# A two-layer graph network on one core: layer 1 in pairs of blocks, another form of the complex products, and the sums of h taken one group earlier

## The chip, the cores and the metric

One core of one Trainium2 chip. The metric is device time in microseconds (us): the median of nine executions, and for the question where the time goes, one profiled execution with a record of every instruction. TensorE (PE in profiles, PEld for its weight loads) multiplies matrices into PSUM, VectorE (DVE) and ScalarE (ACT) read PSUM and do element-wise work, GpSimd (POOL) does element-wise work on SBUF and issues DMAs, SyncE (SP) issues DMAs. Every engine works through its own instructions in the order in which they were recorded, and waits on semaphores for the others.

## The reference, cut to what matters

x is 128 samples x 128 nodes x 256 features, adj a 0/1 adjacency for each sample; all is float32.

```python
# layer 0
h = max(layernorm(x), 0)
y = bn2(conv1d(relu(bn1(conv1_w @ h)), conv2_w, 17 taps, pad 8))   # along the nodes
x_conv = relu(y + h)
s = h @ w_se.T + b_se
x_nmp = (exp(-dist(s, s)) * mask) @ relu(h @ w_msg.T + b_msg)      # mask is adj
gi, gh = [x_conv, x_nmp] @ w_ih.T + b_ih, h @ w_hh.T + b_hh
r, z = sigmoid(gi_r + gh_r), sigmoid(gi_z + gh_z)
n = tanh(gi_n + r * gh_n)
x = x + (1 - z) * n + z * h
# layer 1: five groups of nodes with 25, 9, 7, 6, 6 members, all among nodes 0 to 24
h = max(layernorm(x), 0)
for g, idx in enumerate(GROUPS):
    A = normalised(adj[:, idx][:, :, idx] + I)
    out_g = relu(A @ (relu(A @ (h[:, idx] @ W1[g]) + b1[g]) @ W2[g]) + b2[g])
    x[:, idx] += softmax(fusion_w)[g] * out_g
```

Layer 1 touches only the 25 nodes that are in a group; W1[g] is 256 x 512, W2[g] 512 x 256.

## The kernel before, in words

The 128 samples are worked on in groups of four (q = 0 to 31, `GB` = 4), eight groups make a batch (`bat`, 0 to 3) of layer 0's convolution, and four groups make a block of 16 samples (`blk`, 0 to 7, `SB` = 16) of layer 1.

Layer 0's convolution with 17 taps is done through a Fourier transform over 48 points. `stage_a(q)` normalises four samples, turns them (hT, also written to DRAM as hTd), multiplies with conv1_w (pc, L396) and transforms (pf, L409) into X. `stage_b(bat)` multiplies, for each of 24 frequencies f, the real and imaginary parts of a batch's X with those of the taps. A complex product is made of three real ones: per frequency twelve matmul instructions of 256 columns, two products into the bank pa and one into pb (L500). A float32 matmul is two instructions on TensorE. The taps' transforms come from DRAM (wfd, L486), GpSimd adds the third factors (xs, wf; L494, L495), and after the products ACT copies pa out (pac, L519) and DVE makes real and imaginary part with three operations (L523 to L525). GpSimd writes y to DRAM (yd, L528). The cosines and sines that the taps are multiplied with are the constants of `_fourier` (L89).

`stage_n(q)` loads hT and the adjacency and makes the neighbour sums xm (pse, pm, pd, px: L571 to L616); for the first eight groups this was done early and is only loaded. `stage_c(q)` is the gates: it transforms y back (pi, L673) into xc, and multiplies hT, xm and xc with the gate weights (p, L694) with a fast scheme of seven products for two by two blocks. That scheme needs sums of the quarters of each input: `sums` (L546 to L554) makes four of 256 columns on DVE, th from hT, tm from xm, tc from xc. `stage_c` uses th ready made if `TH` holds it, and makes it at its head otherwise (L665). TH of the next group is made behind the last update with the bank pg (L757 to L760), provided that the next group is in `IN`, that is, that its stage_n is complete. At the end tanh (ACT, L788) and six GpSimd operations (d and z, L791 to L794) give the new state, po (L807) turns it back, and DVE adds it to x. Nodes 0 to 31 of the result go to DRAM for layer 1 (x1d, L819), the others to the output; the last block's stay in SBUF (`direct`, L801).

Layer 1 works on blocks. `prepare(blk)` loads the small adjacency (aj), makes the normalised matrices: b1 with five adds on GpSimd (L917; eight instructions), dg on DVE (L922), pa, pdg, pg and pr4 on TensorE (L928 to L960), giving ac and r4. `rows_of_x` loads x1 (L900), takes moments and normalises (L275 to L283, a power on GpSimd at L278, the maximum with 0 on GpSimd at L894) into x1h. `block(blk)` aggregates (py, L979; yz, L981 and L982), multiplies with W1 of each group (`first`: ph, L996, 16 x members columns) and with W2 (`second`: pz, L1005), turns (pzt, L1026), aggregates again (pg2, L1038), and adds the fused result to x1 (pfu, L1047, L1049); GpSimd stores it (L1058). W1[g] is loaded anew for each block and group with two buffers (L878); W2 is loaded once as a whole (`setup_1`).

The order in which instructions are recorded is planned. Stages are generators: each yields the TensorE time it has just recorded and a delay before it should go on. A `Lane` holds stages with a weight, up to `ahead` of them at a time; `Order.run` always goes on with the lane whose recorded TensorE time, divided by its weight, is smallest, among those that are due. First a lane of stage_a, with tap weights beside it; then stage_b(0); then the lane of gates (stage_n and stage_c, weight 1) beside the remaining stages a and b (0.5); and from there to the end the gates beside layer 1 (L1083). When gates are used up, the rest of layer 1 is recorded alone. Conditions such as `blk - 1 in B1_DONE` concern the recording only. PSUM has three banks for gates (`pgat`) and five for all else (`ptmp`), taken in turn.

```python
    groups = Lane([stage(q) for q in range(NQ) for stage in (stage_n, stage_c)], ahead=2)
    side = Lane(first, weight=0.5)
    order.run(groups, side, until=side)
    order.run(groups, Lane(second, ahead=2, weight=0.4))
```

Of the kernel before, what the change touches and what calls it, by code (L numbers as in the profile page):

```python
# [59 lines left out]
def _fourier():  # L60
# [26 lines left out]
    for f in range(1, NF + 1):  # L87
        th = 2 * np.pi * ((f * t) % F) / F
        tap[:, f], tap[:, NF + 1 + f] = np.cos(th), np.sin(th)  # L89
# [118 lines left out]
def kernel(ctx: ExitStack, tc: tile.TileContext, x, adj, consts, vecs, w_se, conv1_w,  # L208
# [265 lines left out]
    def stage_b(bat):  # L474
# [31 lines left out]
        for f in range(NF + 1):  # L506
            if f + 2 <= NF:
                load_w(f + 2)
            if f < NF:
                add(f + 1)  # L510
            y = xf.tile([P, 2, D], FP, tag="y", name=f"y{bat}_{f}")
            pa = ptmp.tile([P, 2, D], FP, tag="tmp", name=f"pa{bat}_{f}")
            for s in range(2):
                product(pa[:, s], lambda k: X[:, k, 2 * f + s], f, s)
            if f == 0:
                nc.vector.tensor_copy(y, pa)
            else:
                pac = xf.tile([P, 2, D], FP, tag="pac", name=f"pac{bat}_{f}", bufs=2)
                nc.scalar.activation(pac, pa, AF.Copy)  # L519
                pb = ptmp.tile([P, D], FP, tag="tmp", name=f"pb{bat}_{f}")  # L520
                xs = XS.pop(f)
                product(pb, lambda k: xs[:, k], f, 2)
                nc.vector.tensor_sub(y[:, 0], pac[:, 0], pac[:, 1])  # L523
                nc.vector.tensor_add(pac[:, 0], pac[:, 0], pac[:, 1])
                nc.vector.tensor_sub(y[:, 1], pb, pac[:, 0])  # L525
            WF.pop(f)
            if late is not None:
                nc.gpsimd.dma_start(out=yd[bat][:, 2 * f - 2:2 * f], in_=late)  # L528
            late = y
            yield 1.7 if f == 0 else 2.6, 1.0  # L530
# [13 lines left out]
    TH = {}  # L544
# [91 lines left out]
    def stage_n(q):  # L636
        if q < BQ:
# [4 lines left out]
            yield 0.0, 4.0  # L642
        else:
# [3 lines left out]
            yield 0.0, 4.0  # L647
            xm = LATE["fr"].tile([P, 2, 512], FP, tag="xnmp", name=f"xnmp{q}", bufs=2)
# [3 lines left out]
    def stage_c(q):  # L652
# [99 lines left out]
        for dc in range(2):  # L752
# [6 lines left out]
            if dc and q + 1 in IN:  # L759
                TH[q + 1] = sums("th", q + 1, IN[q + 1][0])  # L760
# [64 lines left out]
    S, B1_DONE, P_DONE, Y_DONE = {}, set(), set(), set()  # L825

    def setup_1():
# [13 lines left out]
        S["w2"] = weight(pool, W2, [P, 5, 4, D], "g (k p) o -> p g k o", "w2", nc.sync)  # L841
        S["ac"] = [pool.tile([P, SB // 2, RP], FP, name=f"ac{i}") for i in range(2)]
        r4 = S["r4"] = [pool.tile([P, QS, GB, NR], FP, name=f"r4{i}") for i in range(2)]
        S["yz"] = pool.tile([P, 2, SB, RP], FP, name="yz")
# [29 lines left out]
    def load_w1(n):  # L874

        if n < NBLK * NG:
            S["w1", n] = S["pool"].tile([P, 2, HID], FP, tag="w1", name=f"w1_{n}", bufs=2)
            nc.sync.dma_start(out=S["w1", n], in_=W1[n % NG].rearrange("(k p) o -> p k o", p=P))  # L878

    def rows_of_x(blk, wait=True):  # L880

        ready = all(q in C_DONE for q in range(blk * QS, (blk + 1) * QS))
        if blk in S or not (wait or ready and blk - 1 in Y_DONE):
            return
        while not (all(q in C_DONE for q in range(blk * QS, (blk + 1) * QS))
                   and blk - 1 in Y_DONE):
# [9 lines left out]

    def load_x1(blk):
# [5 lines left out]
    def prepare(blk):  # L903

        while not (blk - 1 in P_DONE and blk - 2 in {-2, *B1_DONE}):
            yield 0.0, 1.0
        pool, pool2, b1 = S["pool"], S["pool2"], S["b1"]
        ac, r4 = S["ac"][blk % 2], S["r4"][blk % 2]
# [3 lines left out]
        if blk not in X1 and all(q in C_DONE for q in range(blk * QS, (blk + 1) * QS)):  # L912
            load_x1(blk)
# [55 lines left out]
    def block(blk):  # L969
        while not (blk in P_DONE and blk - 1 in B1_DONE):  # L970
            yield 0.0, 0.5
        pool, yz, b2row, s2w = S["pool"], S["yz"], S["b2row"], S["s2w"]
        w2, ac, r4 = S["w2"], S["ac"][blk % 2], S["r4"][blk % 2]
        x1, x1h = X1.pop(blk), S.pop(blk)

        for q in range(QS):
            py = ptmp.tile([P, 2, GB, NR], FP, tag="tmp", name=f"py{blk}_{q}")
            for cc in range(2):
                nc.tensor.matmul(py[:, cc], x1h[:, q, cc * P:(cc + 1) * P],  # L979
                                 r4[:, q].rearrange("p j r -> p (j r)"), start=True, stop=True)  # L980
            nc.vector.tensor_copy(yz[:, 0, q * GB:(q + 1) * GB, :NR], py[:, 0])  # L981
            nc.scalar.activation(yz[:, 1, q * GB:(q + 1) * GB, :NR], py[:, 1], AF.Copy)  # L982
            yield 0.75, 0.0 if q < QS - 1 else 1.5
        Y_DONE.add(blk)

        hs = {}

        def first(g):
            n, o = SIZES[g], OFFS[g]
            w1 = S.pop(("w1", blk * NG + g))  # L990
            hh = hs[g] = pool.tile([P, 4, SB, n], FP, tag="hh0" if g == 0 else "hh",
                                   name=f"hh{blk}_{g}", bufs=1 if g == 0 else 2)
            for m in range(4):
                ph = ptmp.tile([P, SB, n], FP, tag="tmp", name=f"ph1{blk}_{g}_{m}")
                for k in range(2):
                    nc.tensor.matmul(ph, w1[:, k, m * P:(m + 1) * P],  # L996
                                     yz[:, k, :, o:o + n], start=(k == 0), stop=(k == 1))
                nc.scalar.activation(hh[:, m], ph, AF.Relu, bias=v("b1", g * 4 + m))

        def second(g):  # L1000
            n, o = SIZES[g], OFFS[g]
            for cc in range(2):
                pz = ptmp.tile([P, SB, n], FP, tag="tmp", name=f"pz1{blk}_{g}_{cc}")
                for m in range(4):
                    nc.tensor.matmul(pz, w2[:, g, m, cc * P:(cc + 1) * P], hs[g][:, m],  # L1005
                                     start=(m == 0), stop=(m == 3))
                nc.vector.tensor_copy(yz[:, cc, :, o:o + n], pz)

        for g in range(NG + 1):
            if g < NG:  # L1010
                first(g)
                yield 5.5 if g == 0 else 1.95, 0.0
            if g:
                second(g - 1)
                yield 5.5 if g == 1 else 1.95, 0.0 if g < NG else 1.0
            if g < NG:
                load_w1(blk * NG + g + 2)
# [3 lines left out]
        def turn(q):  # L1021
            pz = ptmp.tile([P, 2, D], FP, tag="tmp", name=f"pzt{blk}_{q}")
# [6 lines left out]
            zt = zts[q] = pool.tile([P, 2, D], FP, tag="zt", name=f"zt{blk}_{q}", bufs=3)  # L1029
            nc.scalar.activation(zt, pz, AF.Copy)  # L1030

        def gather(q):
            zt = zts[q]
            pg2 = ptmp.tile([P, 2, D], FP, tag="tmp", name=f"pg2{blk}_{q}")
            for a in range(2):
                for s in range(2):
                    rows = slice(s * RP, (s + 1) * RP)
                    nc.tensor.matmul(pg2[rows, a], ac[rows, 2 * q + a], zt[rows, a],  # L1038
                                     start=True, stop=True)
            nc.vector.tensor_tensor(zt, pg2, b2row[:, None, :].to_broadcast([P, 2, D]), ALU.add)  # L1040
            nc.scalar.activation(zt, zt, AF.Relu)

        def fuse(q):
            zt = zts.pop(q)
            pf = ptmp.tile([P, D], FP, tag="tmp", name=f"pfu{blk}_{q}")
# [3 lines left out]
            nc.vector.tensor_add(x1[:, q], x1[:, q], pf)  # L1049

        for what, q in ((turn, 0), (turn, 1), (turn, 2), (gather, 0), (gather, 1), (fuse, 0),
                        (turn, 3), (gather, 2), (fuse, 1), (gather, 3), (fuse, 2), (fuse, 3)):
            what(q)
            if (what, q) == (gather, QS - 1):
                B1_DONE.add(blk)
            yield {turn: 0.45, gather: 0.9, fuse: 0.5}[what], 0.5
        for j in range(GB):
            nc.gpsimd.dma_start(  # L1058
                out=out[blk * SB:(blk + 1) * SB, :WIDE].rearrange("(q j) n c -> j n q c", j=GB)[j],
                in_=x1[j * WIDE:(j + 1) * WIDE])  # L1060
# [17 lines left out]
    for blk in range(NBLK):  # L1078
        second += [prepare(blk), block(blk)]
# [3 lines left out]
    order.run(groups, Lane(second, ahead=2, weight=0.4))  # L1083
# [41 lines left out]
```

## Time and profile before

| | us |
|---|---|
| median of nine executions | 2243.55 (2239.39 to 2257.99) |
| the profiled execution, its own time | 2243.55 |
| its span, first to last instruction | 2241.8 |
| L500, L694 (all inputs): complex and gate products, TensorE busy | the largest groups; 186.0 for pa, 95.4 for pb |
| L996 + L1005, layer 1's products, TensorE busy | 113.1 + 110.1 |
| stretch 2185 to 2242, TensorE busy | 43.12 of 57 |
| W2's load issued | at 1366.4, 2560 KB |

The profile gives for each engine the time in which it was busy. A matmul's record reaches from its start to the modelled end of its results, so neighbouring records overlap; the distance between starts is the pace. In groups of instructions, "out<-in" are the tiles by name, then come partitions x elements, the count, the busy time, the mean of one in ns, and the idle time in front of them with what ended it. The chain of waits goes back from the last instruction to what released each step. Times in the timeline count from the start of the span.

### The profile page before, as it was taken

Reading aid. Unit: us, or ns where it says so; the run is one execution under the profiler, and the core shown is the slowest. Engines: PE = TensorE matmul, PEld = TensorE weight load, DVE = VectorE, ACT = ScalarE, POOL = GpSimd, SP = SyncE. Lnnn points to the kernel's source line nnn. Section 1 sums busy time; section 2 is a strip of 40 time slices with the busy share of each in tenths; the row PEclk is TensorE's granted clock in tenths of the full one; section 3 lists DMA queues with packets and bytes.
Section 4 is the critical chain, followed back from the end, with each engine's and each line's share of the span. In section 5 each row is a group of like instructions: output and inputs, shape, how many; then the busy total and the mean of one; then the engine's idle time right before and its main releaser. Section 6 shows DMA issues by size and latency. Waiting matters only on the chain.

```text
span 2241.8 us, 31926 instructions
## 1 busy us (share of the span) xinstructions
PE 2154.1 (96%) x11820; PEld 1761.6 (79%) x11820; DVE 1337.0 (60%) x2843; ACT 717.9 (32%) x1455; POOL 810.9 (36%) x978
## 2 busy tenths in 40 slices
PE   6998999999999999999999998999999999999997
PEld 3577778888888888888888887787877878878775
DVE  4556656576557676666666665665655665655442
ACT  2432223322234433333333332233333333333232
POOL 2226503365632245542225454423223323222320
PEclk9998989999999999999999999999999999999999
DMA  9786543454533344432315444323212222221221
GB/s 174 234 275 212 187 117 92 133 182 154 158 111 85 104 136 141 147 119 89 103 47 175 137 146 137 77 76 76 76 57 86 65 59 79 80 74 45 69 73 48
DMA packets 193982, 259.72 MB, mean 116 GB/s; under 512 B 21981, under 2 KB 157154, under 8 KB 192290
## 3 DMA queue, kind: packets, MB, share of 16 engines
q1 hardware_dynamic: 165682, 175.89, 27.2%
q0 software_dynamic: 27312, 81.03, 11.7%
q8 instruction: 94, 1.54, 0.3%
q10 hardware_dynamic: 832, 0.75, 0.2%
q14 instruction: 62, 0.51, 0.1%
HBM read 178.44 MB, written 79.17 MB: 115 GB/s over the span
## 4 chain that ended last, share of the span: by engine, by line
PE 83%; DVE 7%; DMA 4%; issue 2%; ACT 2%; POOL 2%; SPq 1%; DVEq 0%; ACTq 0%; POOLq 0%
PE p L694 32%; PE pa L500 7%; PE pg L755 5%; PE pc L396 5%; PE pz L1005 4%; PE ph L996 4%; PE pm L591 4%; PE pi L673 4%; PE pf L409 3%; PE pb L500 3%; PE px L616 2%; DMA hTd<-hTa 1%; PE pg L1038 1%; PE py L979 1%; PE ph L383 1%
## 5 line engine op out<-in xcount | busy, mean ns | idle before, releaser
L500 PE MATMUL pa<-wf,X 128*128 128x256 f32 x768 | 186.0, 386 | 4.8 <-DVE y L525 4.8
L791 POOL TENSOR_TENSOR d<-hT,r 128x512 f32<-128x512 f32 x64 | 86.5, 1351 | 239.2 <-ACT r L788 206.5
L278 POOL TENSOR_TENSOR rs<-rs,cst 128x4 f32<-128x4 f32 x40 | 41.3, 1032 | 358.8 <-DVE rs L277 343.7
L500 PEld LDWEIGHTS pa<-wf,X 128*128 128x128 f32 x768 | 147.3, 193 | 29.8 <-DVE y L525 6.5
L694 PE MATMUL p<-tc,wrz 128*128 128x256 f32 x512 | 152.9, 380 | 4.0 <-DVE tc L551 4.0
L694 PE MATMUL p<-tm,wrz 128*128 128x256 f32 x512 | 152.4, 379 | 1.6 <-DVE tm L551 1.6
L694 PE MATMUL p<-th,wrz 128*128 128x256 f32 x512 | 153.7, 382 | 0.0
L396 PE MATMUL pc<-c1w,hTa 128*128 128x256 f32 x512 | 130.5, 401 | 8.8 <-ACT hTa L385 8.8
L396 PEld LDWEIGHTS pc<-c1w,hTa 128*128 128x128 f32 x512 | 100.1, 200 | 39.2 <-ACT hTa L385 15.9
L495 POOL TENSOR_TENSOR wf<-wf 128x512 f32<-128x512 f32 x92 | 125.3, 1362 | 11.8 <-DMA wf<-wfd 11.8
L494 POOL TENSOR_TENSOR xs<-X 128x256 f32<-128x256 f32 x92 | 69.0, 750 | 165.3 <-PE pb L500 160.6
L673 PEld LDWEIGHTS pi<-cst,yt 96*128 96x128 f32 x1024 | 123.2, 196 | 4.7 <-issue 3.1
L673 PE MATMUL pi<-cst,yt 96*128 96x64 f32 x1024 | 121.9, 278 | 2.7 <-DMA yt<-yd 2.7
L755 PE MATMUL pg<-hT,whn 128*128 128x512 f32 x256 | 122.6, 605 | 0.0
L591 PE MATMUL pm<-wmsg,hT 128*128 128x256 f32 x512 | 121.3, 381 | 0.0
L694 PE MATMUL p<-hT,wrz 128*128 128x256 f32 x384 | 120.4, 396 | 0.0
L519 ACT ACTIVATE pac<-pa 128x512 f32<-128x512 f32 x92 | 54.7, 595 | 197.9 <-PE pa L500 189.3
L523 DVE TENSOR_TENSOR y<-pac 128x256 f32<-128x256 f32 x92 | 55.4, 603 | 102.2 <-ACT pac L519 98.8
L996 PE MATMUL ph<-yz,w 128*128 128x96 f32 (+3 forms) x640 | 113.1, 332 | 3.4 <-DVE yz L981 2.8
L591 PEld LDWEIGHTS pm<-wmsg,hT 128*128 128x128 f32 x512 | 96.4, 190 | 23.8 <-issue 11.0
L694 PEld LDWEIGHTS p<-tc,wrz 128*128 128x128 f32 x512 | 96.8, 190 | 19.3 <-DVE tc L551 6.4
L1005 PE MATMUL pz<-hh,w 128*128 128x96 f32 (+3 forms) x640 | 110.1, 327 | 1.7 <-DVE aT L608 1.7
(205 smaller groups left out, 4818.6 us busy)
## 6 DMA issues: line engine op xcount, KB each, us to landing
wf<-wfd SPq DMA_DIRECT2D x192, 256.0 KB, 3.2
yd<-y POOLq DMA_DIRECT2D x96, 256.0 KB, 2.6
yt<-yd SPq DMA_DIRECT2D x64, 384.0 KB, 3.7
hT<-hTd SPq DMA_DIRECT2D x40, 512.0 KB, 5.3
w<-in_W SPq DMA_DIRECT2D x40, 512.0 KB, 3.8
xa<-in_x SPq DMA_DIRECT2D x128, 128.0 KB, 4.0
hTd<-hTa POOLq DMA_DIRECT2D x32, 512.0 KB, 4.2
xt<-in_x SPq DMA_DIRECT2D x128, 128.0 KB, 3.2
```

The lines of the kernel that those rows point to most:

```text
L396: nc.tensor.matmul(pc[:, i], hT[:, k, (2 * h + i) * N:(2 * h + i + 1) * N], c1w[:, k], start=(k == 0), stop=(k == 1))
L409: nc.tensor.matmul(pf[:, i, :F * NB], h1[:, 2 * h + i, k * P:(k + 1) * P], fwd, start=True, stop=True)
L494: nc.gpsimd.tensor_tensor(XS[f], X[:, :, 2 * f], X[:, :, 2 * f + 1], ALU.add)
L495: nc.gpsimd.tensor_tensor(WF[f][:, :, 2], WF[f][:, :, 0], WF[f][:, :, 1], ALU.add)
L500: nc.tensor.matmul(ps, xk(k), WF[f][:, k, s], start=(k == 0), stop=(k == 1))
L591: nc.tensor.matmul(pm[:, i], hT[:, k, j * N:(j + 1) * N], wmsg[:, k], start=(k == 0), stop=(k == 1))
L673: nc.tensor.matmul(pc[:, co, a * 64:(a + 1) * 64], yt[:, a, co * P:(co + 1) * P], inv[:HB], start=True, stop=True)
L694: nc.tensor.matmul(ps[:, m], w[:, i, k, m * P:(m + 1) * P], factor(i, x, t), start=first and j == 0, stop=last and j == len(n) - 1)
L755: nc.tensor.matmul(pg, whn[:, k, dc * P:(dc + 1) * P], hT[:, k], start=(k == 0), stop=(k == 1))
L791: nc.gpsimd.tensor_sub(d, hT[:, dc], r[:, dc])
L996: nc.tensor.matmul(ph, w1[:, k, m * P:(m + 1) * P], yz[:, k, :, o:o + n], start=(k == 0), stop=(k == 1))
L1005: nc.tensor.matmul(pz, w2[:, g, m, cc * P:(cc + 1) * P], hs[g][:, m], start=(m == 0), stop=(m == 3))
```

## The change

Four things are changed.

1. Layer 1 works on pairs of blocks (`blocks(sb)`, 32 samples). Groups 1 to 4 are multiplied for both blocks at once; group 0, with 25 members, still half by half[...]. W2 is loaded group by group with two buffers, like W1, and both once for each pair. `ac` has three buffers, `yz` is twice as large. An x1 tile is loaded only when the block two before has been fused (`x1_there`), and block k's prepare needs blocks k - 2 aggregated and k - 3 gathered. The store of a block's result stands at its last fuse.
2. The complex products: pa now holds imaginary part times one factor and real part times the other, the constants of `_fourier` are sums and differences of cosine and sine, ACT copies pb (`kk`) and not pa, and one DVE operation makes y = 2 pa - kk.
3. The condition for making th of the next group is that its hT has been requested (`HT`), not that its stage_n is complete.
4. The share of layer 1 beside the gates is 0.48 instead of 0.4 of theirs.

```diff
-        tap[:, f], tap[:, NF + 1 + f] = np.cos(th), np.sin(th)
+        tap[:, f] = -(np.cos(th) + np.sin(th)) / 2
+        tap[:, NF + 1 + f] = (np.sin(th) - np.cos(th)) / 2
...
-                product(pa[:, s], lambda k: X[:, k, 2 * f + s], f, s)
+                product(pa[:, s], lambda k: X[:, k, 2 * f + (s if f == 0 else 1 - s)], f, s)
...
-                pac = xf.tile([P, 2, D], FP, tag="pac", name=f"pac{bat}_{f}", bufs=2)
-                nc.scalar.activation(pac, pa, AF.Copy)
                 pb = ptmp.tile([P, D], FP, tag="tmp", name=f"pb{bat}_{f}")
                 xs = XS.pop(f)
                 product(pb, lambda k: xs[:, k], f, 2)
-                nc.vector.tensor_sub(y[:, 0], pac[:, 0], pac[:, 1])
-                nc.vector.tensor_add(pac[:, 0], pac[:, 0], pac[:, 1])
-                nc.vector.tensor_sub(y[:, 1], pb, pac[:, 0])
+                kk = xf.tile([P, D], FP, tag="kk", name=f"kk{bat}_{f}", bufs=2)
+                nc.scalar.activation(kk, pb, AF.Copy)
+                nc.vector.scalar_tensor_tensor(y, pa, 2.0, kk[:, None].to_broadcast([P, 2, D]),
+                                               op0=ALU.mult, op1=ALU.subtract)
...
+            HT[q] = hT
...
-            if dc and q + 1 in IN:
-                TH[q + 1] = sums("th", q + 1, IN[q + 1][0])
+            if dc and q + 1 in HT:
+                TH[q + 1] = sums("th", q + 1, HT.pop(q + 1))
...
         for n in range(2):
             load_w1(n)
-        S["w2"] = weight(pool, W2, [P, 5, 4, D], "g (k p) o -> p g k o", "w2", nc.sync)
-        S["ac"] = [pool.tile([P, SB // 2, RP], FP, name=f"ac{i}") for i in range(2)]
+            load_w2(n)
+        S["ac"] = [pool.tile([P, SB // 2, RP], FP, name=f"ac{i}") for i in range(3)]
...
+    def x1_there(blk):
+
+        return (all(q in C_DONE for q in range(blk * QS, (blk + 1) * QS))
+                and blk - 2 in {-2, -1, *F_DONE})
...
+        def first(g, half=None):
+
             n, o = SIZES[g], OFFS[g]
-            w1 = S.pop(("w1", blk * NG + g))
+            bs = slice(0, 2 * SB) if half is None else slice(half * SB, (half + 1) * SB)
+            nb = bs.stop - bs.start
+            w1 = S["w1", sb * NG + g]
...
-                                     yz[:, k, :, o:o + n], start=(k == 0), stop=(k == 1))
+                                     yz[:, k, bs, o:o + n], start=(k == 0), stop=(k == 1))
...
+        yield from aggregate(pair[0])
+        yield first(0, 0)
+        yield from aggregate(pair[1])
+        yield second(0, 0)
+        yield first(0, 1)
+        yield first(1)
+        yield second(0, 1)
+        for g in range(2, NG):
+            yield first(g)
+            yield second(g - 1)
+        yield second(NG - 1)[0], 1.0
...
-    for blk in range(NBLK):
-        second += [prepare(blk), block(blk)]
+    for sb in range(NBLK // 2):
+        second += [prepare(2 * sb), prepare(2 * sb + 1), blocks(sb)]
...
-    order.run(groups, Lane(second, ahead=2, weight=0.4))
+    order.run(groups, Lane(second, ahead=2, weight=0.48))
```

## The prediction, made before the result was known

> **What bounds the kernel now.** I read the page's first lines, then the chain of waits, the table by stage, the groups with shapes kept apart, and the timeline of the end.
>
> ```profile
> span 2241.8 us, 31926 instructions
> PE 2154.1 (96%) x11820; PEld 1761.6 (79%) x11820; DVE 1337.0 (60%) x2843; ACT 717.9 (32%) x1455; POOL 810.9 (36%) x978
> PEclk9998989999999999999999999999999999999999
> PE 83%; DVE 7%; DMA 4%; issue 2%; ACT 2%; POOL 2%; SPq 1%; DVEq 0%; ACTq 0%; POOLq 0%
> ```
>
> TensorE is busy nearly everywhere and carries 83% of the chain that ended last. But busy is not pace, so I take the pace from the chain in order of time (start, length, what):
>
> ```profile
> 606.13 10.36 PE p L694 x48
> 1367.72 15.03 DMA hT<-hTd
> 1435.20 5.42 PE ph L996 x16
> 2217.22 3.57 PE pz L1005 x32
> ```
>
> 256 columns take 10.36/48 = 0.216 us an instruction, 400 take 5.42/16 = 0.339, that is 0.843 ns a column; 96 take 3.57/32 = 0.112, not the 0.081 of their columns. The starts of 64, 96, 112 and 128 columns all lie 0.110 to 0.112 apart, those of 144 0.123. So narrow ones sit on a floor. Giving every instruction of the trace its spacing adds up to 2042.5 us. The first matmul starts at 15.8, the last ends 10.7 before the end; what is left, 172.8 us, is stalls and slow clock: 37.8 before 170 us, 32.4 from there to 292 (first complex products), 33.6 to 1358, 12.0 to 1420, 40.0 to 2098 (gates beside layer 1), 16.7 after. The table by stage (stretch, length, then busy PE, PEld, DVE, ACT, POOL, clock, DMA share, GB/s) says the same:
>
> ```profile
> 112.00:224.00 112.00, 99.70 (x597) 80.04 (x590) 71.28 (x141) 33.26 (x77) 51.02 (x58) 0.94 0.75 243
> 448.00:560.00 112.00, 111.61 (x541) 96.06 (x540) 77.63 (x142) 27.36 (x54) 63.40 (x74) 0.98 0.54 170
> 1344.00:1456.00 112.00, 103.01 (x528) 82.90 (x527) 65.88 (x149) 30.78 (x63) 47.83 (x61) 0.95 0.39 107
> 2185.00:2242.00 57.00, 43.12 (x282) 30.08 (x278) 13.27 (x30) 17.05 (x37) 4.44 (x8) 0.93 0.17 47
> ```
>
> So an edit pays only if it removes TensorE pace, or fills one of the holes at the start, at 1370 and at the end.
>
> **What the skill says.** "TensorE: Matmul & The Clock Gate", section LDWEIGHTS: loading weights takes columns/1.2 ns, 107 for 128. That fits the floor of 0.110 to 0.112. Part 1 of that page: an idle window of about 3.4 us halves the clock until it has been busy again; the clock record here has half-speed stretches of 3.4 to 13.7 us after holes, one from 1380.8 to 1387.6. "SBUF — State Buffer", section on the two sides: a VectorE operation with two SBUF inputs and a GpSimd operation hold one port pair in turn, and the loser blocks. The groups agree (count, busy, mean ns):
>
> ```profile
> L552 DVE TENSOR_TENSOR th<-hT 128x256 f32<-128x256 f32 x32 | 39.0, 1218 | 0.0
> L552 DVE TENSOR_TENSOR tm<-xnmp 128x256 f32<-128x256 f32 x24 | 10.8, 452 | 0.0
> L524 DVE TENSOR_TENSOR pac<-pac 128x256 f32<-128x256 f32 x92 | 77.5, 842 | 3.2
> L523 DVE TENSOR_TENSOR y<-pac 128x256 f32<-128x256 f32 x92 | 55.4, 603 | 102.2 <-ACT pac L519 98.8
> ```
>
> The same 256-column operation costs 452 ns for tm and 1218 for th, which stands beside GpSimd's gate arithmetic. One that reads PSUM (L525) stays at 425.
>
> **Part by part.** *Pairs.* Group 0 keeps 400 columns. Groups 1 to 4 had 144, 112, 96, 96 columns on 8 blocks, and get 288, 224, 192, 192 on 4 pairs. At L996 and L1005 alike that is 128 x 0.123 + 128 x 0.112 + 256 x 0.112 = 58.8 us before, and 64 x 0.243 + 64 x 0.189 + 128 x 0.162 = 48.4 after, at 0.843 ns a column. Twice 10.4: **-20.8 us**, all of it on the bounding engine. ACT and DVE evictions halve in count there too; they are hidden by TensorE, so nothing.
>
> *Weights of layer 1.* W2 is no longer one 2560 KB load at 1366; two pieces of 512 KB go ahead, the rest in turn. In the hole at 1358 to 1420 hT's load, queued behind W2 on SP, took 15.0 us and TensorE waited 6.8 for it. 1536 KB less at the 380 GB/s seen in those slices is **-4.1 us** (0 to -7). Later, 20 loads of each weight instead of 40 and 1; each needs the slot of two groups earlier, and SP waits for TensorE to have left it. Behind stand hT, yt, xt and x1 loads, but w lands in a median of 3.8 us and hT is wanted some 40 us later: hidden.
>
> *Products.* TensorE keeps its 12 instructions a frequency. DVE loses 0.603 + 0.842 + 0.425 = 1.87 us, and gets one operation over 512 columns from PSUM, like L757's at 0.748. ACT loses 0.595 and copies 256 columns, 0.35 to 0.50. That is 1.12 x 92 = 103 us off DVE and some 15 off ACT, none of it pace. pa's bank is held longer: its four pb matmuls (0.86), the copy and the DVE operation follow, about 1.4 us more than now; pb's comes free about 1.4 sooner. With five banks in turn I set that at nothing; bounds +6 to -16. The gain must come out of the 32.4 us of stalls at 170 to 292, where waits on DVE's y and ACT's pac held TensorE 12 us and the slow clock, 20.5 us of half speed, cost 10. I take half of the first and a fifth of the second: **-8 us**.
>
> *Sums of h in front.* Four DVE operations in each of 24 groups (8 to 31) move from the head of stage_c, where they run beside GpSimd's d and z, to between L757 and the candidate's products. At 0.45 instead of 748, 1111, 1218, 1217 ns (mean of all 32), DVE wins about 2.5 us a group. At the new place the four delay v2's and r's updates by 1.8 us while seven products of 0.86 us run with three banks: slack enough. hT was requested a group earlier, so no DMA is waited for. At the old place the wait reached TensorE rarely (tc 5.0, xc 3.3, tm 1.7 us in all): **-4 us**, bounds 0 to -10.
>
> *Order and end.* The built order shows where the share 0.48 leaves things. Pairs 0 to 2 lie beside gates; after the last product of group 31 only pair 3 is left, where now three blocks are. But its second block has nothing in front of it. From now's timeline of the end (start, us, engine, line):
>
> ```profile
> 2089.98 1.27 POOL L791 TENSOR_TENSOR d<-hT,r 128x512 f32<-128x512 f32 x1 [12.57 <-ACT r L788]
> 2096.62 1.26 POOL L794 TENSOR_TENSOR z<-d,r 128x512 f32<-128x512 f32 x1
> 2105.90 2.92 POOL L917 TENSOR_TENSOR b<-aj,cst 25x400 f32<-25x400 f32 x8
> 2129.63 1.38 DVE L283 TENSOR_SCALAR x1h<-x,mv,rs 128x256 f32<-128x256 f32 x4 [1.12 <-POOL rs L278]
> 2131.19 3.66 POOL L894 TENSOR_SCALAR x1h<-x1h 128x1024 f32<-128x1024 f32 x1 [1.59 <-PE ph L996]
> ```
>
> Let T be the end of that last product, 2089.3 now. In the new order GpSimd does six d and z operations (to T+8.6), then block 7's b1 (2.9: T+11.5). DVE's dg waits for that, and behind dg stands the fourth eviction of block 6's py, so block 6's first 400-column group starts at T+13 on a cold clock and ends near T+20. po follows (T+21.5), then block 7's pa, ac, dm, moments, x1h, pg, ac, r4, one after another from the same rows: 15 us, py at T+36.7. Then 1.4 + 5.4 + 2 (cold clock) + 35 us of pace to T+80.5, eight turn, gather and fuse steps, 19 (four take 10.6 now), and 10.7 to the end: T+111, of which 67.4 is pace. That is 32.9 us of stall against 20.8 now: **+12 us**, bounds 0 and +25. x1's loads for blocks 2 to 6 wait on SP for the stores of the pair before, with xt and adjacency loads behind them, and DVE's moments wait for x1. The order leaves 12 to 15 us of TensorE work between store and moments; from the first store (L1058) at 2103.7 to the last x1 load landed at 2112.0 that chain takes 8.3 now: nothing, but see the third rival.
>
> *Sum.* -20.8 - 4.1 - 8 - 4 + 12 = -24.9 us. The profiled execution took 2243.55 us, its span 2241.8; 2243.55 is also the median of the nine. So 2218.65, **2219 us**.
>
> **Rivals.** *Relief counts for more.* If a lighter DVE also removes a third of the 33.6 and 40.0 us of stalls and half of the 32.4: -20.8 - 4 - 16 - 25 + 12, about **2190**. For it: DVE holds 7% of the chain. Against: most waits there are single fixed gaps of 0.15 to 0.3 us. *The end takes it back.* If pair 3 stalls by 25 instead of 12 and relief gives 2: -20.8 - 4 - 2 + 25, **2242**, no change. For it: several engines wait in turn there, and DVE has few other things to do. *Slower.* x1's load for blocks 2 to 6 waits on SP for a store, and DVE's moments wait for the load with gate operations behind them. GpSimd issues the stores, and its queue also holds six d and z operations of a group (7.9 us), which wait for tanh. If these get in front, the chain is 16 to 23 us and not 8.3, DVE stands some 8 us five times, and TensorE with it: +40 on top gives about **2259**. It decides as soon as the chain exceeds the 12 to 15 us left. Against: the built order has no d or z directly ahead of these stores.
>
> **How the numbers follow.** Forecast 0.54 (2207 to 2236), more relief 0.22, end takes it 0.16, slower 0.08. The range runs from 2195, inside the relief case, to 2243, which leaves out the slower case, part of the end's and the tip of relief: under 0.2. A measurement of this kernel can tell about 0.3% (6.7 us) from no change: faster 0.80, same 0.11, slower 0.09.
>
> **What would show it.** Right: 32 matmuls of 192 columns at 0.16 us; the wait for hT near 1370 shorter by 4; one DVE operation of 0.7 to 0.8 us a frequency; th at 0.45; some 100 us off DVE's busy time in the products; TensorE idle for over 20 us in two holes about po31. Wrong: spacing of 192 columns still above 0.2; new idle time before moments in the middle; more than 40 us of stall after T.

## The result and the profile after

| | before | after |
|---|---|---|
| median, all runs on the same chips, us | 2247.86 (54 runs) | 2237.08 (17 runs) |
| lowest to highest, us | 2235.92 to 2257.99 | 2225.99 to 2244.50 |
| ratio, 95% interval | | 0.9950 [0.9937, 0.9963] |
| profiled execution, its own time | 2243.55 | 2239.60 |
| its span | 2241.8 | 2237.8 |

The change is worth about 11 us, 0.5%, where 24.9 were forecast. The direction is right and the size is not: less than half came. Ratios from here on are against runs of the kernel before on the same chip, with their 95% interval in brackets.

The page of the changed kernel, the lines that answer to those of before:

```profile
span 2237.8 us, 30548 instructions
PE 2136.5 (95%) x11308; PEld 1734.7 (78%) x11308; DVE 1149.8 (51%) x2627; ACT 687.9 (31%) x1391; POOL 795.1 (36%) x978
PEclk9899989999999999999999999999999999999979
PE 84%; DVE 5%; DMA 4%; POOL 3%; issue 2%; ACT 1%; SPq 1%; DVEq 0%; POOLq 0%; ACTq 0%
L524 DVE SCALAR_TENSOR_TENSOR y<-pa,kk 128x512 f32<-128x512 f32 x92 | 63.6, 692 | 168.2 <-ACT kk L523 162.8
L523 ACT ACTIVATE kk<-pb 128x256 f32<-128x256 f32 x92 | 35.3, 383 | 239.1 <-PE pb L501 239.1
```

TensorE has 512 instructions less and is busy 17.6 us less; DVE is busy 187 us less. The span shrank by 4.0. So most of what DVE gained was not on the path, and part of what TensorE gained was given back. The clock record shows where to look: a 7 in the last slice but one, 2126 to 2182, where before had a 9.

The chain of waits in order of time (start, length, what) has the doubled widths:

```profile
2185.94 3.44 PE ph_None L1014 x16
2195.87 3.03 PE pz_None L1029 x16
2202.36 5.21 PE pz_None L1029 x32
```

3.03/16 is 0.189 us for 224 columns and 5.21/32 is 0.163 for 192, 0.84 to 0.85 ns a column. So pz (L1029, the products with W2) left the floor behind and keeps the pace that was worked out. ph (L1014, the products with W1) does not: 3.44/16 is 0.215 us for 224 columns. From the timeline (start, us, engine, line; a record runs on past the start of the next):

```profile
2185.78 3.61 PE L1014 MATMUL ph_None<-yz,w 128*128 128x224 f32 x16
2195.71 3.19 PE L1029 MATMUL pz_None<-hh_None,w 128*128 128x224 f32 x16
2193.11 2.76 PE L1014 MATMUL ph_None<-yz,w 128*128 128x192 f32 x16
2198.73 3.62 PE L1014 MATMUL ph_None<-yz,w 128*128 128x192 f32 x16
```

No wait stands in any of the four. The sixteen starts of ph with 224 columns are evenly 0.215 us apart, not 0.189. Of ph's two groups with 192 columns one keeps 0.163 and the other takes 0.217, in each of the four pairs; 288 columns keep 0.243. ph gathers its columns out of yz, a few neighbouring ones (as many as the group has members) from each row of 64, while those of pz lie side by side; the two groups with 192 differ only in where in the row these few begin. No run varies that, and the cause stays open. It costs 16 x 0.026 + 16 x 0.054 = 1.3 us a pair, some 5.2 in all.

The table by stage (stretch, length, then busy PE, PEld, DVE, ACT, POOL, clock, DMA share, GB/s):

```profile
112.00:224.00 112.00, 105.51 (x631) 84.82 (x630) 60.80 (x131) 33.39 (x82) 52.56 (x61) 0.94 0.77 250
1344.00:1456.00 112.00, 104.07 (x500) 80.71 (x499) 68.97 (x176) 29.45 (x61) 47.71 (x63) 0.94 0.26 72
2119.90:2238.00 118.10, 82.39 (x383) 56.59 (x381) 28.41 (x70) 24.58 (x49) 26.09 (x35) 0.84 0.15 44
```

In the first products TensorE went from 99.7 to 105.5 busy of 112. The stretch with W2 changed by one. The third row is the end: T, the end of the last gate product, is 2119.9, and the end comes 117.9 later (forecast T+111) at a clock of 0.84.

**Where the time went.** I give every instruction the spacing at which its shape normally follows itself, as in the prediction, and cut the traces at events instead of times: the first pi (end of the first complex products), the last pb (end of the last), and T. What is left over is stall, slow clock and, for the pairs, ph's slower groups; the totals differ by under 2 us from the prediction's.

| us | up to first pi | to last pb | to T | to the end | pace of all |
|---|---|---|---|---|---|
| before | 71.4 | 33.9 | 48.6 | 20.3 | 2040.9 |
| after | 62.0 | 27.1 | 65.5 | 36.3 | 2020.2 |
| difference | -9.4 | -6.8 | +16.9 | +16.0 | -20.7 |

The sum is -4.0, the difference of the two spans. The pace here gives ph the spacing of its columns, so it really fell by some 15.5 us and not by 20.7; the 5.2 us between them stand in the stalls, 3.9 in the third column and 1.3 in the fourth. The first two columns are the products and the sums of h. The third, in which gates lie beside layer 1, is what the prediction set at nothing.

**The end.** The timeline (start, us, engine, line):

```profile
2122.04 1.28 POOL L793 TENSOR_TENSOR d<-hT,r 128x512 f32<-128x512 f32 x1
2128.64 1.26 POOL L796 TENSOR_TENSOR z<-d,r 128x512 f32<-128x512 f32 x1
2129.86 2.93 POOL L928 TENSOR_TENSOR b<-aj,cst 25x400 f32<-25x400 f32 x8
2130.85 0.77 DVE L933 TENSOR_REDUCE dg<-b 25x16 f32<-25x400 f32 x2 [8.24 <-POOL b L928]
2133.42 7.89 PE L1014 MATMUL ph<-yz,w 128*128 128x400 f32 x16 [10.51 <-DVE yz L998]
2150.59 1.04 POOL L279 TENSOR_TENSOR rs<-rs,cst 128x4 f32<-128x4 f32 x1
2153.79 2.05 PE L966 MATMUL pg<-dd,cst 128*128 128x512 f32 x2 [9.45 <-DVE dd L961]
```

This is the queue that the prediction named, at its times: six d and z, then b1, then dg, then the eviction, and the 400-column group starts at T+13.5 (forecast T+13). There are two holes of about 10 us, one in front of this group and one in front of pg. The group takes 7.89 instead of 5.42 and pg 2.05 instead of 0.86: the clock record has half speed from 2127.7 to 2137.9 and from 2144.8 to 2165.3.

**The middle.** TensorE's waits between 1420 and 2089 in the same trace (waiting line, what it waited for, total us, times, longest):

```profile
PE pg L966 <- DVE dd L961: 6.5, 3, 2.8
PE ph L1014 <- ACT yz L999: 3.3, 2, 1.7
PE py L996 <- DVE r L975: 3.1, 3, 1.1
PE pfu L1079 <- DVE zt L1069: 1.9, 2, 1.0
PE pfu L1079 <- DVE aT L608: 1.5, 2, 0.8
```

In before's list for the same stretch, which adds up to 10.5 us where this one has 16.3, ph waits once for an eviction (1.9) and pfu once for aT (0.3); the other three don't occur. Here they come two or three times, about once a pair. One of them near 1630:

```profile
1628.85 3.03 PE L996 MATMUL py<-r,x1h 128*128 128x212 f32 x16
1628.80 2.26 POOL L1084 DMA_DIRECT2D out<-x  x4 [7.18 <-DVE x L1081]
1631.07 2.94 POOL L928 TENSOR_TENSOR b<-aj,cst 25x400 f32<-25x400 f32 x8
1632.09 0.77 DVE L933 TENSOR_REDUCE dg<-b 25x16 f32<-25x400 f32 x2 [1.79 <-POOL b L928]
1634.22 0.93 DVE L998 COPY yz<-py 128x212 f32<-128x212 f32 x3
1635.30 5.66 PE L1014 MATMUL ph<-yz,w 128*128 128x400 f32 x16 [1.66 <-ACT yz L999]
```

GpSimd's b1 of the pair's second block is queued behind four stores of the pair before; dg waits for b1 on DVE; three evictions of the first block's py, whose last product ended at 1631.88, are recorded behind dg. It is the chain of the end, in small. The largest entry, pg for dd, is the second hole of the end in small:

```profile
1668.08 1.02 POOL L279 TENSOR_TENSOR rs<-rs,cst 128x4 f32<-128x4 f32 x1 [10.87 <-DVE rs L278]
1669.13 1.38 DVE L284 TENSOR_SCALAR x1h<-x,mv,rs 128x256 f32<-128x256 f32 x4 [1.13 <-POOL rs L279]
1670.43 0.69 DVE L961 TENSOR_TENSOR dd<-cst,dm 128x512 f32<-128x512 f32 x1
1671.17 1.12 PE L966 MATMUL pg<-dd,cst 128*128 128x512 f32 x2 [1.86 <-DVE dd L961]
```

GpSimd's power rs lets DVE make x1h, dd is recorded behind x1h on DVE, and pg waits for dd. Single gaps of over 0.5 us between 1420 and T add up to some 22 us where before had 11.5. So of the 16.9 us some 10 are these waits and 3.9 are ph's slow groups; the rest isn't located. The column also moves without pairs: the kernel with the sums alone (below) has some 7 us more in it than before, with 44 us at half clock there instead of 20.

### The profile page after: what moved, and what is told of

Its sections match the earlier page's. It is cut to its first block, busy times and chain, and to the rows that moved or that the text cites. A ratio compares the mean times of both kernels' runs of the same rounds, so it can differ in the third digit from the quotient of the medians.

```text
span 2237.8 us, 30548 instructions
## 1 busy us (share of the span) xinstructions
PE 2136.5 (95%) x11308; PEld 1734.7 (78%) x11308; DVE 1149.8 (51%) x2627; ACT 687.9 (31%) x1391; POOL 795.1 (36%) x978
## 4 chain that ended last, share of the span: by engine, by line
PE 84%; DVE 5%; DMA 4%; POOL 3%; issue 2%; ACT 1%; SPq 1%; DVEq 0%; POOLq 0%; ACTq 0%
PE p L696 32%; PE pa L501 7%; PE pg L757 5%; PE pi L675 5%; PE pm L591 4%; PE pc L397 4%; PE pb L501 3%; PE pf L410 3%; PE ph_None L1014 2%; PE px L616 2%; PE pz_None L1029 2%; PE ph L1014 2%; PE pz L1029 2%; PE pg L1067 1%; PE ph L384 1%
## 5 line engine op out<-in xcount | busy, mean ns | idle before, releaser
L793 POOL TENSOR_TENSOR d<-hT,r 128x512 f32<-128x512 f32 x64 | 81.5, 1273 | 311.9 <-ACT r L790 311.9
L524 DVE SCALAR_TENSOR_TENSOR y<-pa,kk 128x512 f32<-128x512 f32 x92 | 63.6, 692 | 168.2 <-ACT kk L523 162.8
L397 PE MATMUL pc<-c1w,hTa 128*128 128x256 f32 x512 | 125.4, 389 | 5.3 <-ACT hTa L386 5.3
L496 POOL TENSOR_TENSOR wf<-wf 128x512 f32<-128x512 f32 x92 | 116.4, 1266 | 15.6 <-DMA wf<-wfd 15.4
L591 PEld LDWEIGHTS pm<-wmsg,hT 128*128 128x128 f32 x512 | 97.9, 193 | 24.4 <-issue 10.4
L709 ACT ACTIVATE r<-r,brz 128x256 f32<-128x256 f32 x128 | 58.1, 500 | 174.7 <-DVE r L737 164.1
L523 ACT ACTIVATE kk<-pb 128x256 f32<-128x256 f32 x92 | 35.3, 383 | 239.1 <-PE pb L501 239.1
L696 PEld LDWEIGHTS p<-tm,wrz 128*128 128x128 f32 x512 | 97.2, 190 | 14.5 <-DVE tm L551 1.3
```

The source lines that it names most:

```text
L397: nc.tensor.matmul(pc[:, i], hT[:, k, (2 * h + i) * N:(2 * h + i + 1) * N], c1w[:, k], start=(k == 0), stop=(k == 1))
L496: nc.gpsimd.tensor_tensor(WF[f][:, :, 2], WF[f][:, :, 0], WF[f][:, :, 1], ALU.add)
L591: nc.tensor.matmul(pm[:, i], hT[:, k, j * N:(j + 1) * N], wmsg[:, k], start=(k == 0), stop=(k == 1))
L696: nc.tensor.matmul(ps[:, m], w[:, i, k, m * P:(m + 1) * P], factor(i, x, t), start=first and j == 0, stop=last and j == len(n) - 1)
L793: nc.gpsimd.tensor_sub(d, hT[:, dc], r[:, dc])
```

## The experiments

My theory, to be tested: the pace came as worked out; the products gave more than forecast; the pairs give back most of their pace, half at the end and half at the two or three junctions in the middle, since a pair's second block has its matrices made only when TensorE already needs them. Rival 1: pairs gain and the form of the products costs. Rival 2: the share of layer 1 (0.48 instead of 0.4 of the gates') places things badly, not the pairs.

**The complex products alone**, on the kernel before: only the second part of the diff.

> The kernel before with the new form of the complex products alone (constants, pa with crossed parts, kk, one DVE operation). Theory A (the lighter DVE is worth what the trace after shows: stalls at 170 to 292 us down 11, some of the 12 less between 292 and 1358): 12 to 18 us faster than before. Rival (TensorE's pace bounds, the relief between traces was chance): within 3 us of before.

Measured 2228.17, 0.9897 [0.9869, 0.9926]: 23 us faster, more than either said. Rival 1 falls. DVE in the window 155 to 292, first in the kernel before, then with this part (count, busy, mean ns, idle before and releaser):

```profile
L523 DVE TENSOR_TENSOR y<-pac 128x256 f32<-128x256 f32 x23 | 23.6, 1026 | 30.0 <-ACT pac L519 26.7 <-DMA yd<-y 3.3
L524 DVE TENSOR_TENSOR pac<-pac 128x256 f32<-128x256 f32 x23 | 15.0, 651 | 0.8
```

```profile
L524 DVE SCALAR_TENSOR_TENSOR y<-pa,kk 128x512 f32<-128x512 f32 x23 | 15.9, 690 | 42.7 <-ACT kk L523 34.2 <-DMA yd<-y 8.4
```

The operation that makes y from two SBUF inputs had a mean of 1026 ns there, where the prediction took 603, its mean over all batches; the one on pac had 651 where it took 842. With the third (425) that is 2.10 us a frequency for the 1.87 of the prediction, only some 5 us over the 23 frequencies. The new operation has twice the columns and takes 690.

**The same form, with both inputs in SBUF**, on the kernel with the products alone. ACT copies pa as well:

```diff
+                pac = xf.tile([P, 2, D], FP, tag="pac", name=f"pac{bat}_{f}", bufs=1)
+                nc.scalar.activation(pac, pa, AF.Copy)
-                nc.vector.scalar_tensor_tensor(y, pa, 2.0, kk[:, None].to_broadcast([P, 2, D]),
+                nc.vector.scalar_tensor_tensor(y, pac, 2.0, kk[:, None].to_broadcast([P, 2, D]),
```

> The kernel before with the new products alone, but ACT copies pa to SBUF too and the one DVE operation reads two SBUF tiles instead of PSUM and SBUF: pa's bank comes free earlier, DVE still has one operation for three, and it can be held up by GpSimd again. Theory A (what the products gain is the DVE operations of 603 and 842 ns that stood behind GpSimd): the operation's mean rises from 0.69 to over 0.9 us and a third or more of the 23 us is given back: 8 to 16 us faster than before. Rival (what counts is one operation instead of three, or the banks): 19 us or more faster than before.

Measured 2238.13, 0.9959 [0.9942, 0.9976]: 9 us faster than before instead of 23.

```profile
L526 DVE SCALAR_TENSOR_TENSOR y<-pac,kk 128x512 f32<-128x512 f32 x92 | 128.0, 1391 | 156.6 <-ACT pac L525 150.6 <-DMA yd<-y 6.1
L526 DVE SCALAR_TENSOR_TENSOR y<-pac,kk x92: 678/1705/3211, 166.2 to 1343.4; 128x512 f32<-128x512 f32 x92
```

The same operation takes 1391 ns where the one that reads PSUM takes 691; the second line gives the shortest, the median and the longest in ns. The Trainium skill ("SBUF — State Buffer", section "SBUF: two separate sides") says that a VectorE operation with two SBUF inputs and a GpSimd operation that reads SBUF exclude each other, and that the one that comes second waits until the first is done. The trace agrees: 19 of the 92 had no GpSimd arithmetic beside them and took 689 ns on average, the other 73 took 1574. So inputs in SBUF aren't slower in themselves. Some 14 of the 23 us, 7 either way, go when pa is read from SBUF. ACT's additional copy of 512 columns is in these 14 as well; the two weren't separated. The single trace shows no stage for them: its stall up to the first pi is 60.7 us, among those of the traces that read PSUM.

**The sums of h alone**, on the kernel before: only the third part of the diff.

> The kernel before with th of the next group made as soon as its hT was requested, nothing else. Theory A: th at 0.42 to 0.45 us instead of 0.75 to 1.2, DVE some 70 us less busy, but few TensorE waits hang on it: 3 to 8 us faster. Rival (those waits are hidden): within 3 us of before.

Measured 2242.88, 0.9979 [0.9964, 0.9993]: 5 us faster, as forecast (4). In the trace the stall between first pi and last pb goes from 33.9 to 28.2. At its new place the third of the four operations for th takes 418 ns, where its mean was 1218:

```profile
L552 DVE TENSOR_TENSOR th<-hT 128x256 f32<-128x256 f32 x32 | 13.4, 418 | 0.0
```

**The pairs alone**, on the kernel before: the first and fourth part of the diff, with W2 in pieces.

> The kernel after without the new products and with th made as before: pairs of blocks, W2 in pieces and the share 0.48 alone. Theory A (pairs take 20.8 us of TensorE pace away and give back 16 at the end and some 19 at the junctions in the middle): 5 to 20 us slower than before. Rival (pairs gain as forecast, what was lost in the trace after lies in the other parts or is chance): 8 to 15 us faster.

Measured 2261.53, 1.0065 [1.0046, 1.0084]: 15 us slower. The trace has 2020.2 of pace, 68.5 of stall up to T and 37.5 after it, against 48.6 and 20.3. TensorE's waits, from 1420 to 2120 and after it:

```profile
PE pg L964 <- DVE dd L959: 6.5, 3, 2.8
PE py L994 <- DVE r L973: 5.4, 4, 2.3
PE ph L1012 <- ACT yz L997: 3.3, 2, 1.7
```

```profile
PE ph L1012 <- DVE yz L996: 10.5, 1, 10.5
PE pg L964 <- DVE dd L959: 9.4, 1, 9.4
```

The same waits at the same junctions are there without the other parts: it is the pairs.

**Products and sums without pairs.**

> The kernel before with the new products and the sums in front, blocks one by one, W2 whole, share 0.40. Theory A (parts add up): 23 + 5 us faster than before, about 0.9875 of it, so faster than after by some 17 us and slower than early matrices by 8. Rival (both relieve the same DVE waits, so they don't add): 0.990 of before, as the products alone.

Measured 2220.09, 0.9885 [0.9860, 0.9910]: 26 us faster. 23 and 5 add up within the intervals, and 23 + 5 - 15 = 13 stands for the 11 of the whole. The change would be better without the part that takes the most work off TensorE.

**Pairs, products in halves.** The changed kernel with all pairs' organisation, but each product of groups 1 to 4 again as two of a block's width (second likewise):

```diff
-                for k in range(2):
-                    nc.tensor.matmul(ph, w1[:, k, m * P:(m + 1) * P],
-                                     yz[:, k, bs, o:o + n], start=(k == 0), stop=(k == 1))
+                for i in range(0, nb, SB):
+                    for k in range(2):
+                        nc.tensor.matmul(ph[:, i:i + SB], w1[:, k, m * P:(m + 1) * P],
+                                         yz[:, k, bs.start + i:bs.start + i + SB, o:o + n],
+                                         start=(k == 0), stop=(k == 1))
```

> The kernel after with the products of groups 1 to 4 again half by half, 16 samples to a matmul, into the same banks and in the same order; junctions, loads and evictions stay those of pairs. Theory A (the wide products alone are worth the 20.8 us of pace): 17 to 24 us slower than after, so about 8 us slower than before. Rival (part of that pace was hidden behind other waits): less than 12 us slower than after.

Measured 2248.61, 1.0014 [0.9996, 1.0032], which is 0.64% or 14 us above the changed kernel, some 5 either way. The pace of its trace is back at 2040.9. 17 to 24 was expected, under 12 by the rival, and the result lies between. It fits the 15.5 us by which the pace fell once ph's slow groups are counted.

**Matrices early.** On the changed kernel: block k's matrices may be made when those of k - 1 are, not when k - 1 has its rows of x; four buffers of ac, and a third stage in the lane:

```diff
+        M_DONE.add(blk)
...
-        while not (blk - 1 in P_DONE and blk - 2 in {-2, *Y_DONE}
-                   and blk - 3 in {-3, -2, *B1_DONE}):
+        while not (blk - 1 in {*P_DONE, *M_DONE} and blk - 2 in {-2, *Y_DONE}
+                   and blk - 4 in {-4, -3, -2, *B1_DONE}):
...
-    order.run(groups, Lane(second, ahead=2, weight=0.48))
+    order.run(groups, Lane(second, ahead=3, weight=0.48))
```

> The kernel after, but a block's matrices (b1, dg, ac, r4) are prepared while the pair before is still worked on: they no longer wait for x1h of the block in front (a set of their own, four ac, three stages of layer 1 at a time, aj with one buffer). Theory A (the lost time is the chain of GpSimd's b1, DVE's dg and what stands behind it at each junction, above all behind the last group): the hole in front of the first 400-column products after the last gates falls from 10.5 us to 7 or less and that in front of pg, 9.5 us, goes; stalls in the middle fall by about 7; 15 to 22 us faster than after. Rival (the junctions only wait for x1 itself): within 4 us of after.

The edit gives aj one buffer as well. Measured 2211.51, 0.9838 [0.9815, 0.9861]: 36 us faster than before and 25 (6 either way) faster than the changed kernel, whose interval it doesn't meet, and rather more than the 15 to 22 expected. Stall up to T falls from 65.5 to 55.0, after T from 36.3 to 25.2. TensorE at the end:

```profile
2126.11 5.59 PE L1015 MATMUL ph<-yz,w 128*128 128x400 f32 x16
2135.19 5.32 PE L997 MATMUL py<-r,x1h 128*128 128x212 f32 x14 [3.50 <-POOL x1h L899]
```

The group of 400 runs near full speed, and between it and the second block's py stands one wait of 3.5 us, for x1h and not for a matrix.

**Only the last block's matrices early.** The same condition for block 7 alone; the lane gets its third stage when pair 2 begins.

```diff
+        last = blk == NBLK - 1
+        while not (blk - 1 in (M_DONE if last else P_DONE) and blk - 2 in {-2, *Y_DONE}
+                   and (last or blk - 3 in {-3, -2, *B1_DONE}) and blk - 4 in {-4, -3, -2, *B1_DONE}):
```

> The kernel after with early matrices for block 7 alone; the junctions in the middle stay as they were. Theory A (end and middle both cost, the end with the two holes of 10 us): 10 to 16 us faster than after, the rest up to early matrices' 25 lying in the middle. Rival 1 (all is lost at the end): 20 us or more faster than after. Rival 2 (all in the middle): within 4 us of after.

Measured 2219.06, 0.9881 [0.9859, 0.9902]: 15 us better than the changed kernel. Stall after T goes from 36.3 to 21.4, before T it stays (66.8). This is the end's price, undone by itself, and it leaves some 10 of the 25, 7 either way, to the middle.

**The share**, three runs: the changed kernel with 0.40, and matrices early with 0.40 and 0.36.

> The kernel after with the old share, 0.40 instead of 0.48, nothing else. In the built order 84 us of TensorE work then lie behind the last gates instead of 67, the turns of pair 2 among them. Theory A (the hole at the end comes from block 7's b1 and dg being recorded right behind the last group's six GpSimd operations, with no TensorE work left to lie beside them): the 10.5 us hole in front of the first 400-column products shrinks or goes, the hole in front of pg stays: 3 to 12 us faster than after. Rival (the share only shifts work, the hole goes with it): within 3 us of after.

Measured 2232.07, 0.9927 [0.9900, 0.9954], 5 us below the changed kernel's median, with intervals that overlap. In its trace the stall after T is 39.1 and before T 63.2, no less than with 0.48; what it gains lies before the first pi (46.8), where the share has no part. The hole of 10.5 us in front of the 400-column group is gone (0.5 us), as my theory had said, and the one in front of pg remains (6.9), but a wait of 11.8 us has come in front of pfu: the hole moved. Rival 2 has nothing for it in the trace, but the median doesn't decide it.

> The version with early matrices with the share 0.40: pair 2's last products and all its turns lie behind the last gates. Theory A (what is left there are waits for x1 of blocks 6 and 7, 6.4 us before pfu and 3.7 before py, which pair 2's turns can cover in part): 2 to 10 us faster than early matrices at 0.48. Rival (block 6's x1 still comes after pair 2's first four fuses, so the wait moves along): within 4 us of it.

> As the one before with the share 0.36: half of pair 2's products lie behind the last gates. Theory A: within 4 us of the share 0.40, since the chain for x1 of block 6 is the same. Rival (more work beside it always helps): 5 us or more faster than at 0.40.

Measured 2222.6, 0.9887 [0.9864, 0.9909], and 2210.9, 0.9836 [0.9807, 0.9864]. A miss: 0.40 is 11 us slower than 0.48, 0.36 equal to it; only what the rival said of 0.36 against 0.40 came. Stall up to T is 61.5, 52.5 and (0.48) 55.0. At the end the longest wait in front of pfu is 10.4 us with 0.40 where 0.48 has 6.2, and that in front of po 7.0 where it has 2.4. A share moves everything that is recorded after it, and which waits fall together isn't monotone in it.

**Moments later**, matrices early and the moments of x1 recorded 12 instead of 6 us of TensorE work behind their load:

```diff
-            yield 0.0, 6.0
+            yield 0.0, 12.0
```

> The version with early matrices at 0.48, with 12 instead of 6 us of planned TensorE time between the load of x1 and the moments made of it. Theory A (DVE stands in front of block 6's and 4's moments until x1 has landed, with the gathers behind it: 6.4 us before pfu at the end, 3.5 in the middle): these two go, 3 to 9 us faster than early matrices. Rival (block 6 then comes later, and the wait moves to py): within 3 us of it.

Measured 2214.45, 0.9872 [0.9840, 0.9904]: no gain. Also a miss; stall up to T is 58.4 against 55.0. At the end the wait in front of pfu fell from 13.2 to 2.5 us in all, as my theory had said, but those in front of py for x1h rose from 3.5 to 7.9, of pg from 1.9 to 6.5 and of po from 2.4 to 4.9: the wait moved, as the rival had said.

## Why the prediction was wrong, by its own steps

| step, us | forecast | in the traces | in the runs |
|---|---|---|---|
| pairs, pace | -20.8 | -15.5 | 14 of it by the halves, 5 either way |
| W2 in pieces | -4.1 | -2 to -5 | not run alone |
| products | -8 | -9 in this trace, -15 in the mean | -23 |
| sums of h | -4 | -6 to -7 | -5 |
| the end, without ph's slow groups | +12 | +15 | 15 by the last block alone |
| junctions in the middle | 0 | +15 to +18, some 10 located | some 10 of it undone by early matrices |
| sum | -24.9 | -4.0, the two spans | -11 |

In the traces W2 and the junctions stand in one column of the table of stalls, so that their shares are worked out and not seen apart.

**The step that failed** is the junction in the middle: the order that "leaves 12 to 15 us of TensorE work between store and moments" was costed at "nothing". It looked at one chain, x1's load behind a store, and that one is in fact short enough. But the change puts the second block's matrices right in front of its use at every pair, as at the end, and the prediction worked out that chain (GpSimd's b1, DVE's dg, evictions behind it) for the end only. The other chain of the end, from the moments over GpSimd's power and x1h to dd, was likewise left out in the middle. There gates fill part of each hole, and 3.4 to 3.9 us of gaps remain at each of six places. The table of stalls has +16.9 there, 13 without ph's slow groups; W2's gain lies in the same column, so that the junctions cost 15 to 18, the end's term over again. The sign named for it, new idle time before moments, was also the wrong one: the new idle time stands before pg, ph, py and pfu.

**A second step** was mis-sized: "at L996 and L1005 alike", with all widths "at 0.843 ns a column". That held at L1005 (pz, now L1029) and not at L996 (ph, now L1014), where two of the four wider groups take 0.215 and 0.217 us instead of 0.189 and 0.163. The pace fell by 15.5 us and not by 20.8.

**The products** were undersized, -8 for some -23 [-29, -17]. The working took "half of the first and a fifth of the second" of 12 us of waits and 10 of clock, all of it in the first products, and used means over all batches, which accounts for some 5 us. The mean stall up to the first pi over all traces with this form reading PSUM is 56.7 (ten traces, 47 to 65); over the three without it (71.4, 68.2, 76.7) it is 72. That is 15. No stage shows the remaining 8 of the median; with single traces 18 us apart for one form either number may be off by chance, and it stays open.

**The end** was right in its mechanism and its chain, and some 3 us too small (its steps also add up to T+110.2 and not T+111): the clock was half speed for longer than was set (7.89 for 5.42, pg and pr 2.05 and 2.08 for the two's pace of 0.86 each), and the stores of the gates' result (2.29 us on GpSimd from 2148.28) stood in front of the power in rs.

**W2**: TensorE's wait for hT near 1370, 6.8 us, is gone. But the stall of 1358 to 1420 fell only from 12.0 to 10.2; block 0's own chain now ends there, with a wait of 2.3 us in front of py. Cut at events, from the last pb to block 0's 400-column group, it fell from some 15 to 10; with the pairs alone the same stretch of time has 6.2. Single traces don't size it any better.

**The sums** were right. Of the signs in "what would show it", th at 0.42 and "over 20 us in two holes" (10.51 and 9.45) came, and the spacing of 0.163 for pz and one of ph's two groups. "More than 40 us of stall after T" didn't come (36.3). The rivals: "the end takes it back" gave 2242 with +25 at the end; what came was near that sum with the giving back in two places. Relief from a lighter DVE was there, in the products, but not the 25 us in the gates.

**The clock.** The prediction puts half speed behind idle windows of about 3.4 us. The record of before has more: half-speed stretches begin at 1118.0 after a wait of 1.92 us and at 1630.0 after one of 1.70, and at 547.9 right behind the 32 instructions of a pi, after no wait at all. What sets these off isn't shown.

**What remains.** Matrices early (0.9838) and the same with the share 0.36 (0.9836) beat the kernel before and the changed one. With the junctions shortened, pairs seem worth some 10 us over products and sums alone (0.9838 against 0.9885; the intervals just overlap, so this isn't shown), about two thirds of their pace. Early matrices without pairs were not run, and might gain some of it. What would have to be covered next are the waits for zt (6.17 us before pfu at the end) and for x1h (3.50). Moments later was one try at the first, and it lengthened the second.

## What to carry to other kernels

A merged stage is priced by its joints: write down, for each place where the next unit starts, which engine's queue holds its preparation and what stands in front and behind, and multiply by the number of units, not only at the end, where the hole is easiest to see. When an in-order engine waits, what is recorded behind it waits too, though its inputs are there. Check a pace that is worked out from columns on each product by itself, since two of the same width ran at 0.163 and 0.217 us here. And take the duration of an operation from the stage that is to gain, not from its mean over the run: the mean of 603 ns was 1026 there, and that of 842 was 651.

## What was not expected of the hardware

One and the same VectorE operation over 512 columns cost 691 ns with one input in PSUM and 1391 with both in SBUF, on average over 92; of the latter, those with no GpSimd arithmetic beside them took 689 and those beside it 1574. TensorE's products with 224 and 192 columns ran at two paces, 0.189 or 0.215 us and 0.163 or 0.217, without a wait and in every pair alike. After a hole of 10.5 us TensorE's group of sixteen 400-column instructions took 7.89 us instead of 5.42, so this hole cost a quarter more than its length. And ten kernels that have the same 1398 TensorE instructions up to the first pi reach it between 267 and 285 us: the spread of this start alone is as wide as that of all 17 runs of the changed kernel (18.5 us).
